# Depthwise convolution taps on rows that are not yet normalized, the wrapping strip first, and the last image's end in quarter blocks

## The chip, the cores and the metric

The kernel runs on one core of a Trainium2 chip. The metric is the device time of one execution in microseconds; the time before is the median of three runs, 4038.18 us (4037.26 to 4040.14). Everything is float32.

The engines are named as in the profile: PE (matrix products), PEld (its weight loads), DVE (vector), ACT (scalar, activation functions), POOL (GpSimd), SP (the queue that issues most DMAs). Each takes its instructions in the order in which the program emitted them, and stands still when the next one has to wait.

## The reference

The input `x` has 16 images of 56 x 56 pixels and 384 channels. Two residual layers follow each other:

```
x = x + window_attention(group_norm(x))       # 7x7 windows, shifted by 3, 12 heads of 32
x = x + depthwise_conv3x3(group_norm(x))      # per channel, zero padding, weights clipped to +-1, then their sign
```

The group norm takes mean and variance over the whole image for each of 32 groups of 12 channels, and has neither scale nor shift of its own. So the second layer of an image needs the attention output of all its rows before its norm is known. The attention rolls the image by 3 rows and columns, so that one strip of 7 rows wraps from the bottom of the image to its top, and masks the window pairs that the roll brought together.

## The kernel before

**Tiling.** Channels lie on the 128 partitions, three blocks of them (`NC = 3`). An image is 8 strips of 7 rows, 392 tokens each. A strip is two units of four windows, so there are 256 units `u`, 16 for an image; the loop is in `all_units` (L1013). Strip `r` of an image begins at row `7r + 3`; so the wrapping one (rows 52 to 55 and 0 to 2) is the last of its image.

**Attention of a unit.** Its heavy pieces are the list of `heavy` (L980): six pieces in each unit, three PE products each. Even units make the values of the next strip (`value`, L513, turned by DVE, L526) and half of its queries and keys (`query_key`, L499); odd ones make the other half, then the output projection of their strip (`project`, L690). Around these pieces lie, in this order of the unit: the sums of exponents (`add_up`, L639), logarithm and inverse on ACT (L678, L679), the product with the values (`attend`, L660), and DVE's divide group (L680, L681, L688). In the middle of the unit the scores of the next unit (L569), DVE's exponent input (`softmax`, L586) and ACT's exponential (L604) follow. The projection's result is added to `x` by DVE (L707), and its statistics for the second norm are taken (L713). PSUM has four banks of tag `mm` for all products and outputs and four for the scores.

**Order of the light work.** Loads, norms and convolution are not in that loop. A planner puts each of their pieces at a time counted in units, a fraction included: `at(when, f, ...)` (L942). The loop emits the pieces due, in order of time, behind the heavy piece whose sixth of the unit they fall into:

```
while light and light[0][0] - u <= (i + 1) / len(todo):
    _, g, a = light.pop(0)
    g(*a)
```

`plan_load` (L963) loads the next image: POOL issues its DMAs (`fetch_halves`, L449; a strip takes 12, the wrapping one 48), DVE turns the strip (L466), ACT sorts it into windows (L478, L481), DVE takes statistics (L482). At the image's end POOL works out its first norm (`norm_gather`, `norm_scale`), which passes through DRAM twice.

**The convolution of an image** runs beside the attention of the next, in six bands of 28 rows by 128 channels (`plan_conv`, L945). The projected rows of a strip go to DRAM (`mid`, 59 wide, issued by POOL, L723, after a small copy that wraps the columns, L719). When the last strip is done, the second norm is worked out on POOL and `center` (L730) turns it into coefficients. From 3 units behind the image's end, a band is taken up every 2.6 units: SP loads it (`band`, L741), ACT writes its normalized rows into a zero-bordered buffer (`pad`, L791) and the centre tap with the residual into an accumulator (`middle`, L821), DVE adds eight taps (`tap`, L827) and turns the sum in blocks of 32 (`turn_sum`, L834), SP stores it (`store`, L841). For the convolution that runs beside the last image the step is 1.95.

**The end.** The last image's convolution has no attention beside it. `plan_last` (L907) waits for its norm, worked out by products on PE (`norm_products`), and then gives four bands of the channel blocks 0 and 1 to DVE as above, and the third block to PE, in four quarters of 14 rows: `convolve` (L848) multiplies the normalized rows with diagonal matrices of the taps, 114 columns at a time, which turns them by token as well. `turn_late` (L887) turns the later DVE bands on PE, and their outputs are issued by SP and ACT.

Of the kernel before, what the change touches and what calls it, by code (L numbers as in the profile page):

```python
# [34 lines left out]
def kernel(  # L35
# [30 lines left out]
    R = W + SHIFT  # L66
    LT = 2 * W
# [17 lines left out]
    bpool = ctx.enter_context(tc.tile_pool(name="xb", bufs=1))  # L85
# [23 lines left out]
    dw_t = const.tile([P, NC, 9], F32, tag="dw", name="dw_t")  # L109
    bias = const.tile([P, 2, NH, 2, T], F32, tag="bias", name="bias")  # L110
# [13 lines left out]
    hps = [const.tile([P, BR + 2, W + 2], F32, tag=f"hp{n}", name=f"hp{n}") for n in range(2)]  # L124

    accs = [const.tile([P, 2 * BR, D], F32, tag=f"o{n}", name=f"o{n}") for n in range(2)]
# [22 lines left out]
    def clear_conv():  # L149
        for t in (*xls, *hps, *accs):  # L150
            nc.gpsimd.memset(t, 0.0)
# [42 lines left out]
    def load_depthwise():  # L194
# [10 lines left out]
        nc.vector.tensor_copy(dw_t, pw[:, : NC * 9].rearrange("p (c t) -> p c t", c=NC))  # L205

    loaded_bias = []

    def load_bias(queue, first_q, last_q, fast):


        if not loaded_bias:
            rel = ypool.tile([P, NC, WIN, R], F32, tag="y", name="rel").rearrange("q c h w -> q (c h w)")[:, : T * NH]
            nc.gpsimd.memset(rel, 0.0)
            loaded_bias.append(rel)
# [15 lines left out]
        mask = ypool.tile([P, NC, WIN, R], F32, tag="y", name="mask").rearrange("q c h w -> q (c h w)")[:, : 2 * T]  # L231
# [80 lines left out]
    def fetch_late():  # L312
# [3 lines left out]
        def place(name, rows, width, at=None):  # L316
# [7 lines left out]
        hp = [  # L324
            place("hp_late", LR + 2, W + 2, xls[1].rearrange("p t c -> p (t c)")),
            place("hp_late2", LR + 2, W + 2),
        ]
        acc = [
            place("acc_late", LR, W + 2, xt.rearrange("p c k d -> p (c k d)")),
            place("acc_late2", LR, W + 2),  # L330
        ]
        for t in (*hp, *acc):
            nc.gpsimd.memset(t, 0.0)
        late_tiles.update(gm=gm, dg=dg, hp=hp, acc=acc)
# [5 lines left out]
    def norm_products(key, gm, meanwhile=()):  # L340
        st = stats.pop(key)
# [24 lines left out]
        for f, n in meanwhile[:1]:  # L366
            f(n)
# [7 lines left out]
        for f, n in meanwhile[1:]:  # L375
            f(n)
# [10 lines left out]
    def late_norm(b):  # L387
        norm_products((1, b), late_tiles["gm"])

    xs = {}  # L390
# [5 lines left out]
    def fetch(s):  # L396
        b, r = divmod(s, NS)
        xl = staging(s)
        first = r * WIN + SHIFT
# [37 lines left out]
    def fetch_halves(s, c):  # L437
# [6 lines left out]
        first = r * WIN + SHIFT  # L444
# [133 lines left out]
    def softmax(u, fast):  # L578
# [4 lines left out]
        if fast:  # L583
# [6 lines left out]
            bias[:, int(s % NS == NS - 1)].rearrange("q (i j) w k -> q i (j w) k", i=HPC),  # L590
# [99 lines left out]
    def project(s, m):  # L690
# [4 lines left out]
        if m == 0:  # L695
            ys[s] = ypool.tile([P, NC, WIN, R], F32, tag="y", name=f"y_{s}")
# [9 lines left out]
        view = ys[s][:, m, :, SHIFT:R]  # L706
# [7 lines left out]
        if m == NC - 1:  # L714
            if b not in mids:
                mids[b] = dram.tile([P, NC, H, R], F32, tag="mid", name=f"mid_{b}")
            del xs[s]
            yt = ys.pop(s)
            nc.gpsimd.tensor_copy(yt[:, :, :, 0:SHIFT], yt[:, :, :, W:R])  # L719
            r0 = r * WIN + SHIFT  # L720
            n = min(WIN, H - r0)
            queue = nc.sync if s == B * NS - 1 else nc.gpsimd
            queue.dma_start(mids[b][:, :, r0 : r0 + n, :], yt[:, :, 0:n, :])  # L723
            if n < WIN:
                queue.dma_start(mids[b][:, :, 0 : WIN - n, :], yt[:, :, n:WIN, :])
# [4 lines left out]
    def center(b, pool=nc.gpsimd):  # L730

        coef = coefs[1, b]
        cen = small.tile([P, NC, 2], F32, tag="cen", name=f"cen_{b}")
        pool.tensor_tensor(cen[:, :, 0], coef[:, :, 0], bo_sb, ALU.mult)
        pool.tensor_tensor(coef[:, :, 1], coef[:, :, 1], cen[:, :, 0], ALU.add)
        pool.tensor_tensor(cen, coef, dw_t[:, :, 4].unsqueeze(2).to_broadcast([P, NC, 2]), ALU.mult)
        pool.tensor_scalar(cen[:, :, 0], cen[:, :, 0], 1.0, None, ALU.add)
        pool.tensor_tensor(cen[:, :, 1], cen[:, :, 1], bo_sb, ALU.add)
        centers[b] = cen

    def band(b, k, c):  # L741
# [3 lines left out]
        xb = bpool.tile([P, BR + 2, R], F32, tag="xb", name=f"xb_{b}_{k}_{c}")  # L745
        nc.sync.dma_start(xb[:, at : at + hi - lo, :], mids[b][:, c, lo:hi, :])
        bands[b, k, c] = (xb, at, hi - lo)

    last_strip = ((0, (NS * WIN + SHIFT) % H), ((NS - 1) * WIN + SHIFT, H))

    def band_late(b, k, c, part):

        rows = LR if c == NC - 1 else BR
        lo, hi = max(k * rows - 1, 0), min((k + 1) * rows + 1, H)
        first = k * rows - 1
        if part == 0:
            size = (rows + 2) * R
            if c == NC - 1:
                xb = xpool.tile([P, NC, ST], F32, tag="x", name=f"xb_late_{k}").rearrange("p c n -> p (c n)")
            elif (k, c) == (0, 1):  # L760
                xb = qk.rearrange("p m n -> p (m n)")
            elif (k, c) == (1, 0):
                xb = bias.rearrange("p v h w n -> p (v h w n)")
            else:
                xb = bpool.tile([P, BR + 2, R], F32, tag="xb", name=f"xb_{b}_{k}_{c}").rearrange("p h w -> p (h w)")
# [10 lines left out]
    def pad(b, k, c, late=False):  # L776
# [10 lines left out]
        if k == 0:  # L787
            nc.gpsimd.memset(hp[:, 0, :], 0.0)
# [385 lines left out]
```

## Time and profile before

| what | us |
|---|---|
| median of the runs shown | 4038.18 |
| the profiled execution's own time | 4038.97 |
| its span, first to last instruction | 4037.2 |
| PE busy | 3956.5 |
| DVE busy | 3494.4 |
| ACT busy | 2228.2 |
| POOL busy | 1863.1 |
| last mean of the second norm begins (L345) | at 3945.45 |

Busy time is the union of an engine's instructions. In a row of a timeline the first number is the start in us from the span's start, the second the time from the first to the last of the instructions merged in it; in brackets stand the idle time ahead of it and what ended it. In a row by stretches the engines' busy times stand in the order PE, PEld, DVE, ACT, POOL, then the granted clock of PE, the share of the DMA engines and GB/s.

### The profile page before, as it was taken

Reading aid. Unit: us, or ns where it says so; the run is one execution under the profiler, and the core shown is the slowest. Engines: PE = TensorE matmul, PEld = TensorE weight load, DVE = VectorE, ACT = ScalarE, POOL = GpSimd, SP = SyncE. Lnnn points to the kernel's source line nnn. Section 1 sums busy time; section 2 is a strip of 40 time slices with the busy share of each in tenths; the row PEclk is TensorE's granted clock in tenths of the full one; section 3 lists DMA queues with packets and bytes.
Section 4 is the critical chain, followed back from the end, with each engine's and each line's share of the span. In section 5 each row is a group of like instructions: output and inputs, shape, how many; then the busy total and the mean of one; then the engine's idle time right before and its main releaser. Section 6 shows DMA issues by size and latency. Waiting matters only on the chain.

```text
span 4037.2 us, 144682 instructions
## 1 busy us (share of the span) xinstructions
PE 3956.5 (98%) x63189; PEld 2416.3 (60%) x63189; DVE 3494.4 (87%) x3730; ACT 2228.2 (55%) x4678; POOL 1863.1 (46%) x3159
## 2 busy tenths in 40 slices
PE   7999999999999999999999999999999999999987
PEld 5665555555566565555655556565655655656657
DVE  4656989899898998989899898998989899898897
ACT  3545556556565655556556565655556556565542
POOL 5454545455453554545455453564545455452000
PEclk9999999999999999999999999999999999999998
DMA  4323545454554554545454554554545454553444
GB/s 106 79 70 87 116 104 120 105 126 103 113 120 101 124 113 103 116 104 122 105 126 104 114 119 100 125 112 103 115 109 118 106 124 107 111 119 81 114 104 104
DMA packets 802161, 439.35 MB, mean 109 GB/s; under 512 B 671478, under 2 KB 752023, under 8 KB 801518
## 3 DMA queue, kind: packets, MB, share of 16 engines
q1 hardware_dynamic: 712580, 270.46, 30.8%
q0 software_dynamic: 87648, 159.12, 16.6%
q8 instruction: 498, 8.16, 0.9%
q14 instruction: 145, 1.19, 0.1%
q10 hardware_dynamic: 1290, 0.42, 0.0%
HBM read 170.08 MB, written 158.45 MB: 81 GB/s over the span
## 4 chain that ended last, share of the span: by engine, by line
PE 38%; issue 19%; POOL 17%; DVE 14%; DMA 7%; ACT 2%; SPq 1%; DVEq 0%; POOLq 0%; ACTq 0%
PE pq L502 15%; POOL xl L449 12%; PE py L699 8%; PE pv L515 8%; DVE o L827 6%; PE score_banks L569 3%; PE po L660 2%; DMA mvd<-mv 2%; DMA xl<-in_x_dram 2%; PE score_banks L639 2%; DVE e L586 2%; DVE xt L466 1%; POOL dev L287 1%; DMA gt<-mvd 1%; DMA cod<-both 1%
## 5 line engine op out<-in xcount | busy, mean ns | idle before, releaser
L502 PE MATMUL pq<-xn,wq_t 128*128 128x392 f32 x4608 | 1584.9, 496 | 0.0
L449 POOL DMA_DIRECT2D xl<-in_x_dram x1980 | 1329.1, 726 | 148.0 <-DVE xt L466 96.2
L827 DVE SCALAR_TENSOR_TENSOR o<-hp,dw_t,o 128x1568 f32<-128x1568 f32 x752 | 1378.1, 1833 | 5.4
L502 PEld LDWEIGHTS pq<-xn,wq_t 128*128 128x128 f32 x4608 | 845.4, 188 | 595.9 <-ACT o L821 0.4
L515 PE MATMUL pv<-xn,wq_t 128*128 128x392 f32 x2304 | 815.0, 497 | 13.6 <-DVE y L707 13.6
L699 PE MATMUL py<-ot,wo_t 128*128 128x392 f32 x2304 | 817.9, 500 | 8.2 <-DVE ot L688 7.5
L509 ACT COPY qk<-pq 128x392 f32<-128x392 f32 x768 | 367.4, 482 | 565.5 <-PE pq L502 565.3
L719 POOL COPY y<-y 128x63 f32<-128x63 f32 x128 | 57.1, 446 | 1236.7 <-DVE y L707 1236.7
L699 PEld LDWEIGHTS py<-ot,wo_t 128*128 128x128 f32 x2304 | 425.0, 190 | 311.5 <-DVE ot L688 26.2
L515 PEld LDWEIGHTS pv<-xn,wq_t 128*128 128x128 f32 x2304 | 423.9, 188 | 312.9 <-DVE y L707 15.7
L604 ACT ACTIVATE e<-e 128x1176 f32<-128x1176 f32 x256 | 303.2, 1184 | 499.7 <-DVE e L586 498.8
L680 DVE SCALAR_TENSOR_TENSOR ln<-score_banks,inv 128x588 f32<-128x588 f32 x256 | 195.8, 765 | 322.6 <-ACT inv L679 321.9
L522 ACT COPY vt<-pv 128x392 f32<-128x392 f32 x384 | 188.6, 491 | 366.6 <-PE pv L515 365.9
L569 PEld LDWEIGHTS score_banks<-qk 32*49 32x49 f32 x24576 | 265.8, 118 | 145.3 <-issue 113.5
L586 DVE SCALAR_TENSOR_TENSOR e<-score_banks,bias 128x1176 f32<-128x1176 f32 x256 | 347.0, 1355 | 5.9 <-PE score_banks L569 5.9
L660 PEld LDWEIGHTS po<-e,v 49*32 49x32 f32 x24576 | 311.2, 105 | 51.6 <-issue 2.0
L478 ACT COPY x<-xt 128x196 f32<-128x196 f32 x720 | 225.5, 368 | 176.6 <-DVE xt L466 176.5
L660 PE MATMUL po<-e,v 49*32 49x49 f32 x24576 | 309.9, 212 | 1.0 <-issue 1.0
L569 PE MATMUL score_banks<-qk 32*49 32x49 f32 x24576 | 298.0, 218 | 3.1 <-DVE ln L680 3.1
L526 DVE STREAM_TRANSPOSE vq<-vt 128x512 f32<-128x512 f32 x384 | 265.5, 693 | 8.1 <-ACT vt L522 4.9
L491 ACT ACTIVATE xn<-x,coef 128x392 f32<-128x392 f32 x384 | 247.0, 711 | 4.4 <-DVE coef L381 4.4
L707 DVE TENSOR_TENSOR y<-py,x 128x392 f32<-128x392 f32 x384 | 213.2, 555 | 41.3 <-PE py L699 37.8
(174 smaller groups left out, 3307.6 us busy)
## 6 DMA issues: line engine op xcount, KB each, us to landing
v<-vq SPq DMA_DIRECT2D x2048, 48.0 KB
xb<-mid SPq DMA_DIRECT2D x90, 855.5 KB
out_dram<-o SPq DMA_DIRECT2D x736, 98.0 KB
mid<-y POOLq DMA_DIRECT2D x112, 619.5 KB
xl<-in_x_dram POOLq DMA_DIRECT2D x1260, 52.5 KB
mid<-y POOLq DMA_DIRECT2D x15, 354.0 KB
xl<-in_x_dram POOLq DMA_DIRECT2D x180, 28.0 KB
mid<-y POOLq DMA_DIRECT2D x15, 265.5 KB
```

What stands on the lines that cost most here:

```text
L449: nc.gpsimd.dma_start(xz[i * D + lo : i * D + hi, c, k : k + n, :], flat[token : token + n * (hi - lo)].rearrange("(k t) c -> t k c", k=n) ...
L491: nc.scalar.activation(xn[:, c, :, :T], xs[s][:, c, :].rearrange("p (w t) -> p w t", t=T), AF.Identity, bias=coef[:, c, 1:2], scale=coef[: ...
L502: nc.tensor.matmul(pq[:, :ST].rearrange("p (w t) -> p w t", t=T), wq_t[:, c, m * P : (m + 1) * P], xn[:, c, :, :T], start=(c == 0), stop=( ...
L509: nc.scalar.copy(qk[:, m, :ST], pq[:, :ST])
L515: nc.tensor.matmul(pv[:, :ST].rearrange("p (w t) -> p w t", t=T), wq_t[:, c, 2 * C + m * P : 2 * C + (m + 1) * P], xn[:, c, :, :T], start= ...
L526: nc.vector.transpose(vq[:, :, :, m].rearrange("p h n d -> p n h d"), vt[:, m].rearrange("p (n w) (j b) -> p n (w j) b", w=2, b=D),)
L569: nc.tensor.matmul(pp[row * HT : row * HT + rows, i, k0 : k0 + T], qk[part, NC * fast + j, q0 : q0 + rows], qk[part, NC * (not fast) + j, ...
L586: nc.vector.scalar_tensor_tensor(e, pp[:, :, : NC * 2 * T].rearrange("q i (n k) -> q i n k", k=T), QSCALE, bias[:, int(s % NS == NS - 1)]. ...
L604: nc.scalar.activation(flat, flat, AF.Exp, accum_out=reach[:, 0, u : u + 1])
L660: nc.tensor.matmul(po[w][i * D : (i + 1) * D, (2 * j + r) * T : (2 * j + r + 1) * T], vs[s][keys, i, n * 2 + r, j], by_head(u)[keys, i * N ...
L699: nc.tensor.matmul(py[:, :ST], wo_t[:, c, m * P : (m + 1) * P], ots[s][:, c, :], start=(c == 0), stop=(c == NC - 1),)
L827: nc.vector.scalar_tensor_tensor(acc, by_half(hp[:, dy : dy + BR, dx : dx + W]), dw_t[:, c, t : t + 1], acc, ALU.mult, ALU.add)
```

## The change

Three things change together.

**Taps before the norm.** A convolution of normalized rows is the norm's scale times the convolution of the raw rows, plus the shift times the sum of the taps that fall inside the image. So DVE now adds taps on the raw band, while the norm isn't known yet. `begin` (ACT) writes tap 0 times the raw rows, seven `tap`s follow on DVE, `middle` (ACT, in place in the band) puts in centre tap, residual and the constant, and `edges` (POOL, three small additions for each band) takes off the constants of the taps that fall outside the image. `finish` (DVE) adds the scaled sum to this and turns it, in one call. The rows in `mid` are now 60 wide with zero columns at both sides, so that the padded copy isn't needed; the band pool has two buffers for one, and there are three accumulators for two.

The first band of an image is now planned 1.3 units before the image's end, not 3 after it; centre, edges and finish come where the norm is ready (1.9 units after the end, or behind the taps). The step is 2.6 units, and 1.85 for the later bands beside the last image.

**The wrapping strip first.** Strip `r` now begins at row `7(r-1) + 3`, so the wrapping strip is the first of its image, and the first bands are complete before the image is. The mask goes with it (`s % NS == 0`), and so do the 48 DMA issues of its load.

**The end.** The last image's convolution is in quarters of 14 rows for all channel blocks. The taps of the first three quarters run before the last attention unit is done: blocks 0 and 1 on DVE, block 2 on PE, in 48 steps of 392 columns that are spread over gaps (17 of them planned in the last two units). The last strip isn't written to DRAM, but copied into the last quarter by ACT. What remains after the norm is centre, edges, finish or join, and the output of twelve pieces, each turned on PE and copied out by ACT, with the last quarter's taps in between.

At the start the tap sums for the edges are worked out by DVE (eight small instructions), and the weights are staged in other buffers.

```diff
     def norm_products(key, gm, meanwhile=()):
...
-        for f, n in meanwhile[1:]:
-            f(n)
+        for f, *args in meanwhile[1:]:
+            f(*args)
...
+    def first_row(s):
+        return (s % NS - 1) % NS * WIN + SHIFT
...
-            nc.gpsimd.tensor_copy(yt[:, :, :, 0:SHIFT], yt[:, :, :, W:R])
-            r0 = r * WIN + SHIFT
+            nc.gpsimd.tensor_copy(yt[:, :, :, 1 : 1 + SHIFT], yt[:, :, :, W + 1 :])
+            nc.gpsimd.memset(yt[:, :, :, 0 : W + 2 : W + 1], 0.0)
+            if s == B * NS - 1:
+                late_tiles["rows"] = yt
+                return
+            r0 = first_row(s)
...
+    def begin(b, k, c):
+
+        outs[b, k, c] = accs[count[0] % len(accs)]
+        count[0] += 1
+        xb = bands[b, k, c]
+        nc.scalar.activation(sum_of(b, k, c), by_half(xb[:, 0:BR, 0:W]), AF.Identity, scale=dw_t[:, c, 0:1])
...
+    def centered(b, c, xb, rows):
+
+        cen = centers[b][:, c]
+        here = xb[:, 1 : 1 + rows, 1 : 1 + W]
+        nc.scalar.activation(here, here, AF.Identity, bias=cen[:, 0:1], scale=cen[:, 9:10])
+
+    def edged(b, c, xb, rows, top, bottom):
...
+            nc.gpsimd.tensor_tensor(here, here, by.to_broadcast(shape), ALU.add)
+
+        put(xb[:, 1 : 1 + rows, 1 : 1 + W : W - 1], 3, [P, rows, 2])
+        for side, row, n in ((top, 1, 0), (bottom, rows, 1)):
+            if side:
+                put(xb[:, row, 1 : 1 + W], 1 + n, [P, W])
+                put(xb[:, row, 1 : 1 + W : W - 1], 5 + 2 * n, [P, 2])
...
+    def finish(b, k, c):
+
+        acc, xb = sum_of(b, k, c), bands.pop((b, k, c))
+        nc.vector.scalar_tensor_tensor(
+            acc, acc, coefs[1, b][:, c, 0:1], by_half(xb[:, 1 : 1 + BR, 1 : 1 + W]), ALU.mult, ALU.add
+        )
         flat = outs[b, k, c].rearrange("p h w -> p (h w)")
         nc.vector.transpose(flat, flat)
...
+        at(first - 1.7, convolve, 4)
+        at(first - 1.3, convolve, 9)
+        at(first - 0.9, convolve, 4)
...
+        next_(convolve, 4)
+        next_(norm_products, (1, B - 1), late_tiles, ((convolve, 2), (taps, 0, (1, 2, 3))))
+        next_(center, B - 1, nc.vector)
+        next_(convolve, 9)
...
     def plan_conv(p, first, step, lead, late, queue):
...
-        first += lead
-        for n in range(NB * NC):
+        whens = [first + lead]
+        for n in range(1, NB * NC):
+            whens.append(whens[-1] + (2.6 if n < 3 else step))
+        ready = first + 1.9
+        for n, when in enumerate(whens):
             k, c = divmod(n, NC)
-            when = first + step * n
-            at(max(when - 1.22 * step, first - lead + 0.5), band, p, k, c)
-            at(when - 0.35 * step, pad, p, k, c)
-            at(when - 0.25 * step, middle, p, k, c)
-            for i, t in enumerate((0, 1, 2, 3, 5, 6, 7, 8)):
-                at(when + step * i / 9, tap, p, k, c, t)
-            at(when + step * 8 / 9, turn_sum, p, k, c)
+            end = when + step * 7 / 8
+            fin = max(end + 0.75, ready + 0.5)
+            at(max([when - 1.22 * step] + [f + 0.05 for f in freed[-2:-1]]), band, p, k, c)
+            freed.append(fin)
+            at(when - 0.3 * step, begin, p, k, c)
+            for i, t in enumerate((1, 2, 3, 5, 6, 7, 8)):
+                at(when + step * i / 8, tap, p, k, c, t)
+            at(max(end + 0.25, ready), middle, p, k, c)
+            at(max(end + 0.3, ready + 0.05), edges, p, k, c)
+            at(fin, finish, p, k, c)
...
-            plan_conv(b - 1, NU * b, 2.6 if b < B - 1 else 1.95, 3, 0.4, nc.gpsimd)
+            plan_conv(b - 1, NU * b, 2.6 if b < B - 1 else 1.85, -1.3, 0.4, nc.gpsimd)
```

## The prediction

> **What bounds the kernel now.** I read the busy time by stretches first: two steady images, the last image, and the end after the last attention unit.
>
> ```profile
> 1243.00:1486.00 243.00, 241.19 (x3908) 145.06 (x3907) 219.75 (x230) 139.27 (x293) 118.94 (x206) 1.00 0.50 112
> 3200.00:3443.00 243.00, 241.60 (x3910) 145.25 (x3909) 220.27 (x232) 138.96 (x293) 123.06 (x207) 1.00 0.51 113
> 3686.00:3929.00 243.00, 235.33 (x3983) 142.62 (x3982) 219.78 (x208) 124.86 (x226) 28.04 (x54) 0.99 0.42 97
> 3946.00:4037.20 91.20, 70.76 (x562) 69.96 (x562) 69.45 (x59) 25.34 (x28) 2.56 (x8) 0.82 0.37 81
> ```
>
> The columns after the length are PE, PEld, DVE, ACT and POOL. In a steady image PE is busy 241 of 243 us, so the 14 middle images have at most some 2 us each to give. DVE is busy 220 of 243 us: it is second, with little room, and what matters is when its work comes. At the end nobody is full; 91 us pass there, and this is where the change can gain.
>
> Next the timeline of PE and of DVE over one odd unit (it starts at 2273.90, where the sums of exponents begin) and the start of the even one behind it.
>
> ```profile
> 2273.90 0.72 PE L639 MATMUL score_banks<-e,ones 49*32 49x294 f32 x16
> 2279.66 2.14 PE L699 MATMUL py<-ot,wo_t 128*128 128x392 f32 x6
> 2289.02 0.72 PE L639 MATMUL score_banks<-e,ones 49*32 49x294 f32 x16
> 2291.65 4.22 PE L515 MATMUL pv<-xn,wq_t 128*128 128x392 f32 x12 [0.97 <-DVE y L707]
> ```
>
> ```profile
> 2276.33 0.77 DVE L680 SCALAR_TENSOR_TENSOR ln<-score_banks,inv 128x588 f32<-128x588 f32 x1 [0.98 <-ACT inv L679]
> 2278.01 0.77 DVE L688 TENSOR_TENSOR ot<-ot,ln 128x588 f32<-128x588 f32 x1
> 2278.70 1.84 DVE L827 SCALAR_TENSOR_TENSOR o<-hp,dw_t,o 128x1568 f32<-128x1568 f32 x1
> 2280.46 1.67 DVE L466 STREAM_TRANSPOSE xt<-xl 128x1440 f32<-128x1440 f32 x1
> 2285.33 1.36 DVE L586 SCALAR_TENSOR_TENSOR e<-score_banks,bias 128x1176 f32<-128x1176 f32 x1
> 2291.04 0.56 DVE L707 TENSOR_TENSOR y<-py,x 128x392 f32<-128x392 f32 x1
> ```
>
> They give three times by which DVE must have done something, or PE stands. In an odd unit the divided output (L688) is wanted at +5.8 us, when the projection starts (2279.66). In an even unit the third y must be written at +1.6 us, since the second value product takes its bank; here it came at 2291.60, +2.6, and PE stood 0.97. In every unit the exponent input (L586) must start by about +12.4: it started at 2285.33, its exponential ended at 2288.0, and the next unit began at 2289.0 with 1.0 to spare. Over this image the unit lengths are 14.9 to 15.1 us, save 15.9, 15.7 and 16.1 in the units 2, 5 and 8: 2.7 us of such standing.
>
> **The change, steady state.** Per band the work stays: before, 8 taps, a transpose and two ACT passes; after, 7 taps, a scaling of the same shape in the finish, the transpose, and two ACT passes. DVE's total is unchanged: 0. What changes is **when**: the transpose (2.0) and the finish (1.8) come as one block of 3.8 us, 0.75 units behind the taps, and the taps lie 0.325 units apart, not 0.289. I set out DVE's queue with starts from the rows above: tap 1.8 (2278.70 to 2280.46; eight of one kind took 15.06, so up to 1.89), turn of a loaded strip 1.6, exponent input 1.3, divide group 2.4, v turn 0.65, y 0.57, statistics 0.5.
>
> Unit 3: the exponent input of unit 2 starts at +8; behind it finish 3.8, strip turn, v turn, two taps, two statistics make 12.0 with itself, so the divide starts at +4.9 and ends at +7.3: PE waits 1.5. Unit 4: +2.4, divide, two statistics, two v turns, a tap and a finish put the exponent input at 12.7: 0.3. Unit 5: two taps, v turn and strip turn behind a late exponent input end the divide at +6.95: 1.15. Unit 7: a finish ahead of it, 5.95 and then 12.7: 0.3. Unit 8: third y at +2.6: 1.0. Unit 10: finish, y, tap, y behind the input of unit 9 put the third y at +4.0: 2.4. Sum 6.65.
>
> Two waits come on top. ACT's centre pass of the first band is queued at +1.9 units, right behind the input copies that end at 2289.5, and needs all of the centre coefficients; these were ready only at 2292.2:
>
> ```profile
> 2290.28 0.89 POOL L734 TENSOR_TENSOR cen<-coef,bo_sb 128x3 f32<-128x3 f32 x1 [1.74 <-DMA coef<-cod]
> 2291.91 1.76 ACT L791 ACTIVATE hp<-xb,coef 128x1624 f32<-128x1624 f32 x1
> ```
>
> One tap fewer stands ahead of the mean on DVE, so I expect 2290.7; behind ACT wait the v copy and the logarithm, for which DVE's divide waits. The divide of unit 2 then starts 3.3 us late, and unit 3 pays between 0 and 3.3: I take 1.0. The edge additions of the fifth band are queued on POOL behind the next image's norm chain, and DVE's finish waits for them: 0 to 1.2 in unit 12, I take 0.5. So 8.15, less the 2.7 there now: **5.5 us per image**, bounds 4.0 and 8.5. Loads and a convolution meet in 14 images: **+77** (56 to 119).
>
> At nothing: the band loads (they land 4 to 6 us after their issue in the trace, and the tightest has 8 before ACT's first tap), the wider rows (60 for 59), and the wrapping strip's 48 POOL issues, which move to the image boundary, where POOL is idle (28 us, 0.59 each); were this cover gone, the y copies and edges behind them would be up to 28 us late. One rule speaks against the edges. Each band has three POOL additions. The nearest row is POOL's copy at the same place:
>
> ```profile
> L719 POOL COPY y<-y x128: 235/247/1881, 111.9 to 3945.0; 128x63 f32<-128x63 f32 x128
> ```
>
> Its mean is 446 ns, so three are 1.3 us, inside the 0.45 units (6.8 us) between edges and finish, with 1.7 of ACT's pass. The Trainium skill (SBUF — State Buffer, Who interferes with whom) says that a DVE instruction with two SBUF inputs and a GpSimd instruction that reads SBUF exclude each other for the whole instruction; the 1881 is about a tap's length, so the trace agrees. Were each edge to wait for a whole tap, three would take 6.2, the finish would be 1.1 late, and 84 finishes cost 92. By the row 0; I take the row.
>
> **The change, last image.** Units 240 to 256 now hold some 56 taps and 7.5 transposes. After: 38 taps, 6 finishes and 42 half-size taps. Half of 1833 is 0.92; from the 588-element row (765) 0.97: 0.97 taken. That is 133 for 117, so DVE is at 236 of 243. After the last divide 11 half taps (11 us) lie between and ahead of the last three y, where DVE stood idle: the mean of the last norm, now at 3945.45, comes 7 us later, and the bursts add 5. **+12** (3 to 20). The 17 early convolution steps (0.69 each, two records of 0.344) fill PE's standing time of units 254 and 255 (3.2, 6.4 and 3.0 us).
>
> **The change, end.** From mean to end it takes 91.7 us now:
>
> ```profile
> 3945.45 0.81 DVE L345 BATCH_NORM_AGGREGATE mv<-st 128x2 f32<-128x48 f32 x3
> 3955.20 0.16 DVE L735 TENSOR_TENSOR coef<-coef,cen 128x3 f32<-128x3 f32 x1
> 3958.02 15.06 DVE L827 SCALAR_TENSOR_TENSOR o<-hp,dw_t,o 128x1568 f32<-128x1568 f32 x8
> 4027.48 0.94 ACTq L905 DMA_DIRECT2D out_dram<-xo  x2
> ```
>
> 10 us of norm, four DVE bands of 17, outputs, 10 to the end. After, counted from the mean: coefficients at 10.1, centre at 11.3. PE does nine steps to 14.8, two outputs (1.75 each) to 18.4, eight steps to 23.9, four outputs to 31, the last eight steps to 36.5. Only then may ACT centre the third quarter's last channels in place; with the next pass and its edges the fourth quarter's first finish is at 40.8. Four taps and a join to 46.1, output 48.4, centre and edges 50.4, finish 51.5, five taps 56.7, centre, edges, finish 59.9, output 62.1, DMA and end 7; 2 more for edges that meet taps: 71. **-21** (-12 to -31). DVE alone would need 33, so the order across engines sets it.
>
> **Sum.** 4037.2 (span) + 77 + 12 - 21 = 4105; the start's eight small DVE instructions add at most 1.5 beside loads, taken as 0.5; the median is 1.0 above the span: **4107**.
>
> **Rivals.** (1) The bursts are absorbed, so it is **faster**: DVE waits for ACT's inverse 322 us in all, and any such wait that shortens soaks up a burst. Then 0 + 7 - 23 (edges short): 4022. It turns at 1.1 us per image, 16 over 14. (2) Edges and ACT's hold cost in full, 8.5 per image or more: 4037 + 119 - 9 + 1 = 4148. (3) The end does not shorten, since two banks are held by partial sums until the first join: 4037 + 77 + 12 + 1 = 4127. Against it: most outputs come after that join.
>
> **How the numbers follow.** Likeliest 0.62 (its own range 4065 to 4135), rival 1 0.22, (2) 0.07, (3) 0.04, and 0.05 for small costs that cancel the end's gain. A measurement can tell about 0.2%, 8 us. Faster 0.22, same 0.05, slower 0.73. Leaving out the tails beyond 4148 and some of rival 1: 4020 to 4148.
>
> **What would show it.** Units 3, 5 and 10 of each image longer than 15.1, with waits of the projection for L688's successor and of values for y; ACT waiting for POOL's centre once an image; an image of about 247 us; mean to end near 71. An image of 242 would show the likeliest wrong.

## The result

| what | before | after |
|---|---|---|
| median, us | 4037.72 (4036.82 to 4040.14, 4 runs) | 4140.64 (4138.24 to 4144.1, 4 runs) |
| span of the profiled execution, us | 4037.2 | 4142.3 |
| an image, mean of images 2 to 14, us | 242.0 | 250.0 |
| start of unit 240 to the last mean, us | 235.1 | 250.2 |
| last mean to the end, us | 91.7 | 65.9 |

The changed kernel is slower: 1.0252 of the time before, 95% interval 1.0239 to 1.0265. An image is counted from the first sum of exponents (L637) of its first unit to that of the next image; images and units of an image are counted from 0. The difference of the two spans, 105.1 us, divides into 1.3 at the start, 114.6 in the images 0 to 14 (2.3 of it in image 0), 15.1 up to the last mean, and -25.9 from there to the end.

The busy time by stretches, for one steady image (5), for the last image up to its mean, and for the end; columns as in the prediction.

```profile
1352.00:1602.00 250.00, 241.44 (x3904) 144.32 (x3903) 220.73 (x230) 137.40 (x292) 132.00 (x233) 1.00 0.48 110
3826.20:4076.40 250.20, 238.55 (x3791) 142.28 (x3790) 224.62 (x227) 118.61 (x219) 26.28 (x82) 0.98 0.40 101
4076.40:4142.30 65.90, 36.04 (x168) 25.36 (x168) 38.10 (x61) 26.41 (x42) 9.04 (x25) 0.75 0.28 75
```

PE has as much to do in an image as before (241 us), and DVE too (221 us for 220). The eight microseconds are PE standing still. What PE and its helpers wait for, in the view of waits (total, number, longest, in us), the changed kernel:

```profile
ACT x L476 <- DVE xt L464: 284.2, 114, 5.3
...
PE py L697 <- DVE ot L686: 74.7, 69, 1.9
...
ACT xb L783 <- DVE o L775: 35.5, 15, 2.9
...
DVE o L809 <- POOL xb L792: 28.6, 26, 2.8
...
PE pq L500 <- ACT qk L507: 18.2, 14, 1.8
...
PE score_banks L637 <- ACT e L602: 16.1, 28, 6.0
```

The first of PE's lines, the projection waiting for the divided output, was 7.5 us in all before. A wait of the query product for ACT's copy (L507) was not on the list before. Two lines are of a kind that the kernel before did not have: ACT's centre pass in place (L783) waits for the band's last tap, and DVE's finish (L809) waits for POOL's edges. The first of these two is in unit 11 of every image. In image 9 it looks like this (the unit starts at 2497.06 and the next one, without a wait of PE, at 2513.28):

```profile
2503.09 0.77 DVE L686 TENSOR_TENSOR ot<-ot,ln 128x588 f32<-128x588 f32 x1
2503.91 2.24 PE L697 MATMUL py<-ot,wo_t 128*128 128x392 f32 x6 [1.05 <-DVE ot L686]
2505.72 1.73 ACT L783 ACTIVATE xb<-xb,cen 128x1568 f32<-128x1568 f32 x1 [2.33 <-DVE o L775]
```

ACT begins to wait 6.3 us into the unit. The divide for which PE stands got its inverse from ACT before that, and PE waits for nothing more in this unit, so this wait of ACT costs PE nothing. The waits for edges lie in the units 12 and 14, 0.7 and 1.2 us per image.

By unit, mean of images 2 to 14, in us:

| unit | 2 | 3 | 5 | 7 | 8 | 9 | 10 | 11 | 13 | others |
|---|---|---|---|---|---|---|---|---|---|---|
| before | 16.0 | 15.1 | 15.6 | 15.1 | 15.1 | 15.5 | 14.9 | 15.1 | 15.0 | 14.9 to 15.1 |
| after | 14.9 | 18.8 | 16.3 | 16.0 | 15.0 | 15.2 | 15.7 | 16.4 | 16.2 | 14.9 to 15.3 |

Nearly half of the loss is unit 3. Here it is in image 9, from 2369.92 on, first PE:

```profile
2369.92 0.73 PE L637 MATMUL score_banks<-e,ones 49*32 49x294 f32 x16
...
2371.99 4.22 PE L500 MATMUL pq<-xn,wq_t 128*128 128x392 f32 x12 [0.40 <-ACT qk L507]
2378.08 3.28 PE L697 MATMUL py<-ot,wo_t 128*128 128x392 f32 x6 [1.88 <-DVE ot L686]
2381.29 1.47 PE L567 MATMUL score_banks<-qk 32*49 32x49 f32 x96
```

and DVE and ACT of the same unit, DVE from a little before its start:

```profile
2365.17 1.83 DVE L809 SCALAR_TENSOR_TENSOR o<-o,coef,xb 128x1568 f32<-128x1568 f32 x1
2367.04 2.05 DVE L813 STREAM_TRANSPOSE o<-o 128x1792 f32<-128x1792 f32 x1
2369.01 1.64 DVE L464 STREAM_TRANSPOSE xt<-xl 128x1440 f32<-128x1440 f32 x1
2370.57 0.67 DVE L524 STREAM_TRANSPOSE vq<-vt 128x512 f32<-128x512 f32 x1
2371.16 1.81 DVE L775 SCALAR_TENSOR_TENSOR o<-xb,dw_t,o 128x1568 f32<-128x1568 f32 x1
2372.88 1.03 DVE L480 BATCH_NORM_STATS2 st<-x 128x6 f32<-128x392 f32 x2
2373.83 1.83 DVE L775 SCALAR_TENSOR_TENSOR o<-xb,dw_t,o 128x1568 f32<-128x1568 f32 x1
2375.58 0.76 DVE L678 SCALAR_TENSOR_TENSOR ln<-score_banks,inv 128x588 f32<-128x588 f32 x1
...
2377.26 0.77 DVE L686 TENSOR_TENSOR ot<-ot,ln 128x588 f32<-128x588 f32 x1
```

```profile
2370.68 0.63 ACT L476 COPY x<-xt 128x196 f32<-128x196 f32 x2 [3.75 <-DVE xt L464]
2371.34 0.21 ACT L479 COPY x<-xt 128x21 f32<-128x21 f32 x1
2371.45 0.48 ACT L507 COPY qk<-pq 128x392 f32<-128x392 f32 x1
```

DVE is behind: a band's finish and transpose, 3.9 us, stand ahead of the strip turn that ACT wants, which is done only at 2370.6, and two taps and two statistics stand ahead of the divide, which ends 8.1 us after the unit's start, where 5.8 was the time by which PE wants it. ACT passes the lateness on by another way: its strip copies stand at the head of its queue for 3.75 us, and the query copy behind them, which frees a bank for PE, comes late too (PE's waits in unit 3 are 1.75 us for the divide and 1.26 for that copy, mean of images 2 to 14).

### The profile page after: what moved, and what is told of

Read it like the earlier page. It is cut to its first block, busy times and chain, and to the rows that moved or that the text cites. A ratio compares the mean times of both kernels' runs of the same rounds, so it can differ in the third digit from the quotient of the medians.

```text
span 4142.3 us, 144415 instructions
## 1 busy us (share of the span) xinstructions
PE 3963.5 (96%) x62837; PEld 2380.3 (57%) x62837; DVE 3526.0 (85%) x3780; ACT 2217.3 (54%) x4698; POOL 2008.5 (48%) x3591
## 3 DMA queue, kind: packets, MB, share of 16 engines
q0 software_dynamic: 87680, 160.49, 16.2%
## 4 chain that ended last, share of the span: by engine, by line
DVE 32%; PE 31%; issue 11%; DMA 8%; POOL 7%; ACT 7%; SPq 2%; DVEq 0%; POOLq 0%; ACTq 0%
DVE o L775 10%; PE pq L500 9%; PE py L697 9%; PE pv L513 6%; DMA xl<-in_x_dram 3%; DVE xt L464 3%; DVE e L584 3%; DVE o L809 3%; PE score_banks L567 2%; POOL xl L447 2%; DVE vq L524 2%; DVE st L480 2%; DVE ln L679 2%; DVE st L711 2%; PE po L658 2%
## 5 line engine op out<-in xcount | busy, mean ns | idle before, releaser
L500 PE MATMUL pq<-xn,wq_t 128*128 128x392 f32 x4608 | 1588.3, 497 | 18.4 <-ACT qk L507 18.2
L500 PEld LDWEIGHTS pq<-xn,wq_t 128*128 128x128 f32 x4608 | 847.0, 188 | 617.0 <-ACT qk L507 20.6
L775 DVE SCALAR_TENSOR_TENSOR o<-xb,dw_t,o 128x1568 f32<-128x1568 f32 x630 | 1157.1, 1837 | 1.8
L697 PE MATMUL py<-ot,wo_t 128*128 128x392 f32 x2304 | 827.4, 504 | 77.1 <-DVE ot L686 74.7
L507 ACT COPY qk<-pq 128x392 f32<-128x392 f32 x768 | 359.3, 483 | 546.1 <-PE pq L500 545.9
L717 POOL COPY y<-y 128x63 f32<-128x63 f32 x128 | 33.5, 262 | 796.0 <-DVE y L705 796.0
L480 DVE BATCH_NORM_STATS2 st<-x 128x6 f32<-128x392 f32 x360 | 199.7, 560 | 81.9 <-ACT x L479 81.5
L792 POOL TENSOR_TENSOR xb<-xb,cen 128x56 f32<-128x56 f32 (+1 forms) x270 | 156.8, 581 | 226.9 <-ACT xb L783 212.4
```

The lines of the kernel that those rows point to most:

```text
L480: nc.vector.bn_stats(stats[0, b][:, c, r, :], xs[s][:, c, :])
L500: nc.tensor.matmul(pq[:, :ST].rearrange("p (w t) -> p w t", t=T), wq_t[:, c, m * P : (m + 1) * P], xn[:, c, :, :T], start=(c == 0), stop=( ...
L507: nc.scalar.copy(qk[:, m, :ST], pq[:, :ST])
L697: nc.tensor.matmul(py[:, :ST], wo_t[:, c, m * P : (m + 1) * P], ots[s][:, c, :], start=(c == 0), stop=(c == NC - 1),)
L775: nc.vector.scalar_tensor_tensor(acc, by_half(xb[:, dy : dy + BR, dx : dx + W]), dw_t[:, c, t : t + 1], acc, ALU.mult, ALU.add)
```

## Experiments: which part of the change costs

All times are medians; ratios are to the kernel before, run on the same chip beside each group of experiments (4038.6 to 4039.0). The first four undo or isolate one part each.

**The wrapping strip first, alone, in the kernel before.**

```diff
+    def first_row(s):
+        return (s % NS - 1) % NS * WIN + SHIFT
...
-        first = r * WIN + SHIFT
+        first = first_row(s)
...
-            bias[:, int(s % NS == NS - 1)]
+            bias[:, int(s % NS == 0)]
```

> The kernel before, with the wrapping strip first and nothing else changed: its load with 48 issues moves on POOL's queue from the middle of the image to its end, and the mask with it. Queue theory: DVE's order does not change, so 4034 to 4042. Theory of the wrapping strip (the load stands in the way of what POOL and ACT do at the image's end): a good part of the 8 us per image, 4070 to 4140.

Measured: 4039.2, ratio 1.0001 (0.9992 to 1.0010); an image takes 242.1 us. Moving the strip, its mask and its 48 POOL issues costs nothing that can be measured.

**The edges left out.**

```diff
-            at(max(end + 0.3, ready + 0.05), edges, p, k, c)
```

> The changed kernel, with the three edge additions on POOL left out for all bands that run beside attention (those of the end stay), so the output is wrong at the image borders. POOL theory (edges and DVE shut each other out, and the finish waits for them): most of the 8 us per image goes, 4030 to 4070. Queue theory: only the fifth band's wait behind the norm chain goes, some 1 us in units 12 and 13 of 14 images, so 4115 to 4135, and unit 3 stays near 18.8 us.

Measured: 4130.02, ratio 1.0224 (1.0207 to 1.0241); an image 249.2 us. The edges are worth some 10 of the 103 us (0.8 us per image; the intervals of the two ratios just overlap, so the size is rough). In this trace no finish of the bands beside attention waits for POOL or for ACT, and yet unit 3 takes 18.9 us, and PE's wait for the divide is what it was:

```profile
PE py L697 <- DVE ot L686: 72.2, 70, 1.9
```

So at least 7.2 of the 8.0 us per image are not a wait of DVE for the edges or the centre pass.

**Finish and transpose apart.**

```diff
             at(fin, finish, p, k, c)
+            at(fin + 0.3, turn_sum, p, k, c)
```

> The changed kernel, with the block transpose taken out of the finish and planned 0.3 units behind it, so that other DVE work can come between the two. Queue theory (what counts is how much DVE work stands between two deadlines of PE, not whether it is in one piece): most of the sum stays on the same side of the same deadlines, so 249 to 251 us per image and 4125 to 4155 in all. Block theory (the 3.8 us in one piece is what holds the divide and the exponent input): 243 to 245 per image, 4050 to 4075. POOL theory (the edge additions hold DVE): no change, 4141.

Measured: 4148.0, ratio 1.0267 (1.0250 to 1.0285); an image 250.6, unit 3 even 19.7. The block of 3.8 us as such isn't it.

**DVE's work spread evenly.** Taps 0.289 units apart as before the change, the finish 0.52 units behind the last tap (1.08 in the change), the transpose 0.26 units behind it, and all bands at equal distances. The run also moves the first band, from 1.3 units ahead of the image's end to 0.7 behind it, and the centre pass, from 0.5 to 0.3 units ahead of the finish.

```diff
-        whens = [first + lead]
-        for n in range(1, NB * NC):
-            whens.append(whens[-1] + (2.6 if n < 3 else step))
+        whens = [first + lead + step * n for n in range(NB * NC)]
...
-            fin = max(end + 0.75, ready + 0.5)
+            fin = max(when + 2.25 * step / 2.6, first + 2.4)
...
+            at(fin + step / 10, turn_sum, p, k, c)
```

> The changed kernel, with the steady bands planned at nine even places as before the change: seven taps 0.289 units apart, the finish at the eighth place, the transpose alone at the ninth, the first band 0.7 units after the image's end (0.1 beside the last image, step 1.9). Queue theory: unit lengths as before the change, 241 to 244 us per image; beside the last image DVE has more to do, so the end gains little: 4025 to 4050. POOL theory and theory of the wrapping strip: edges and order of strips are as in the changed kernel, so still 248 to 251 per image and 4125 to 4150.

Measured: 4108.23, ratio 1.0173 (1.0156 to 1.0190); an image 247.0. A third of the loss goes, two thirds stay. So the order of DVE's work matters, but a queue that is only badly ordered would have given much more. One thing got worse here: ACT waits 56.0 us for last taps at the centre pass, for 35.5 in the changed kernel. In this run unit 9 is the longest (17.9 us), with waits of PE for ACT's query copy; that pointed at ACT.

## Experiments: is it ACT that passes the loss on?

**ACT's strip copies later,** in the changed kernel and in the spread one. The first norm's exchange on POOL had to move with them, since it needs their statistics.

```diff
-                at(when + 0.2 + 0.2 * c, arrange, s, c)
+                at(when + 0.6 + 0.2 * c, arrange, s, c)
...
-        at(when + 0.8, norm_gather, (0, b), nc.gpsimd)
-        at(when + 0.9, norm_scale, (0, b), nc.gpsimd)
+        at(when + 1.05, norm_gather, (0, b), nc.gpsimd)
+        at(when + 1.15, norm_scale, (0, b), nc.gpsimd)
```

> The changed kernel with one edit: ACT's copies of a turned input strip are issued 0.4 units (6 us) later, so that they no longer stand at the head of ACT's queue while DVE's strip turn is late; DVE's order is not touched. If a good part of the loss reaches PE through ACT (the copies wait for the strip turn, the query and key copies and the logarithm wait behind them), the waits of the projection products for ACT's query copy go, unit 3 shrinks from 18.8 us to 17.0 to 17.5 and the time is 4100 to 4128. If DVE's queue alone sets the loss, the divide comes no earlier and the time stays within 8 us of the changed kernel: 4133 to 4149.

> The spread order of the experiment before (taps, finish and transpose at even distances, 4108) with ACT's copies of a strip 0.4 units later as well. If what was left there is the relay through ACT (unit 9 mainly: 2.9 us per image), the time is 4060 to 4085 and unit 9 falls from 17.9 us to below 16. If DVE's queue alone sets it, 4100 to 4116.

Measured: 4237.59 (1.0491, 1.0473 to 1.0508) and 4221.55 (1.0452, 1.0431 to 1.0472). Neither theory had that. In the first of the two, PE's waits for the query copy are gone, as meant, but the projection's wait for the divide grew (78.0 us in all for 74.7, the longest 2.8 for 1.9) and unit 3 stays at 18.6: there the relay through ACT took nothing that DVE's lateness would not have taken. Most of the hundred microseconds on top are another matter: unit 12 takes 20.6 us, for 15.2 before the edit, 5.4 in each image. The timeline of image 9, unit 12 of this run, POOL and DVE:

```profile
2575.76 0.79 POOL L313 DMA_DIRECT2D coef<-cod  x1 [1.37 <-DMA cod<-both]
2576.58 0.95 POOL L792 TENSOR_TENSOR xb<-xb,cen 128x56 f32<-128x56 f32 x3
```

```profile
2577.56 1.85 DVE L809 SCALAR_TENSOR_TENSOR o<-o,coef,xb 128x1568 f32<-128x1568 f32 x1 [6.72 <-POOL xb L792]
2579.44 2.04 DVE L813 STREAM_TRANSPOSE o<-o 128x1792 f32<-128x1792 f32 x1
2581.41 1.26 DVE L524 STREAM_TRANSPOSE vq<-vt 128x512 f32<-128x512 f32 x2
2582.60 1.34 DVE L584 SCALAR_TENSOR_TENSOR e<-score_banks,bias 128x1176 f32<-128x1176 f32 x1
```

The fifth band's edges stand on POOL behind the norm exchange of the next image. Moved back by a quarter of a unit and with later statistics, that exchange ends so late that DVE's finish stands 6.72 us for the edges; the exponent input behind it starts at 2582.60, 18.4 us into the unit, and PE stands 6.13. In the changed kernel the same wait is 0.82 us long. In the spread order with late copies DVE waits for edges 188.9 us in all.

## Experiments: the centre pass in place

**DVE in the order of the kernel before.** Bands at the former phase, the finish where the eighth tap was, the transpose where it was; everything else as in the changed kernel. A second run had ACT's copies late as well.

```diff
-            fin = max(when + 2.25 * step / 2.6, first + 2.4)
+            fin = max(when + step * 7 / 9, first + 2.4)
...
-            at(max(fin - 0.3, first + 1.9), middle, p, k, c)
+            at(max(fin - 0.2, first + 1.9), middle, p, k, c)
...
-            at(fin + step / 10, turn_sum, p, k, c)
+            at(fin + step / 9, turn_sum, p, k, c)
...
-            plan_conv(b - 1, NU * b, 2.6 if b < B - 1 else 1.9, 0.7 if b < B - 1 else 0.1, ...)
+            plan_conv(b - 1, NU * b, 2.6 if b < B - 1 else 1.9, 0.4 if b < B - 1 else 0.1, ...)
```

(The lines with a minus are those of the spread run.)

> DVE gets the order of the kernel before: bands at the same phase, seven taps 0.289 units apart, the finish where the eighth tap was, the transpose behind it. ACT's centre pass stays in place, 0.2 units ahead of the finish. If the order of DVE's work is the whole loss of the steady state, an image takes 242 to 243.5 us again and the time is 4025 to 4050, below the kernel before by the gain at the end. If the centre pass in place costs by itself (ACT waits for the last tap of the band, and what is queued on ACT behind it waits too), an image takes 245 to 247 us and the time is 4065 to 4095, with PE waits for ACT's copies in the units of a last tap.

> The run with DVE's former order, and ACT's copies of a strip 0.4 units later. With that order the strip turn comes when it came before the change, so the queue theory expects no difference to that run beyond 8 us. The theory that ACT relays the loss expects a gain of 10 to 30 us, if that run still shows PE waits for ACT's query and key copies behind the strip copies.

Measured: 4145.93 (1.0265, 1.0248 to 1.0282) and 4154.12 (1.0284, 1.0267 to 1.0301). An image takes 248.9 us with the very order that gave 242.0 before. So the former order does not give the former time as long as the centre pass is in place; the second theory was right in kind, and too small in size. But the loss is no longer the changed kernel's: it has moved to the units 0, 5, 7, 8 and 15, and unit 3 is at 15.3. Image 9, unit 15 of the first of the two, from 2549.19 on; ACT, POOL, DVE and PE:

```profile
2555.93 1.72 ACT L783 ACTIVATE xb<-xb,cen 128x1568 f32<-128x1568 f32 x1 [2.23 <-DVE o L775]
```

```profile
2555.89 3.55 POOL L447 DMA_DIRECT2D xl<-in_x_dram  x5 [0.39 <-DMA mid<-y]
2559.46 1.02 POOL L792 TENSOR_TENSOR xb<-xb,cen 128x56 f32<-128x56 f32 x3
```

```profile
2553.99 1.85 DVE L775 SCALAR_TENSOR_TENSOR o<-xb,dw_t,o 128x1568 f32<-128x1568 f32 x1
2560.52 1.85 DVE L809 SCALAR_TENSOR_TENSOR o<-o,coef,xb 128x1568 f32<-128x1568 f32 x1 [4.68 <-POOL xb L792]
...
2563.37 1.36 DVE L584 SCALAR_TENSOR_TENSOR e<-score_banks,bias 128x1176 f32<-128x1176 f32 x1
```

```profile
2566.10 0.73 PE L637 MATMUL score_banks<-e,ones 49*32 49x294 f32 x16 [1.47 <-ACT e L602]
```

This is the chain that the change made: the last tap ends on DVE, only then may ACT centre the rows in the buffer that the tap has read, only then may POOL put in the edges (and here it is in the middle of issuing loads), only then may DVE finish. From the tap's end at 2555.8 to the finish DVE stands 4.68 us, and everything behind the finish with it: the exponent input starts 14.2 us into the unit. In all, ACT waits 121.3 us for last taps in this run and DVE 125.5 us for edges (35.5 and 28.6 in the changed kernel). So this run shows what the chain costs when the finish stands close behind the taps; it does not show that the changed kernel pays for it.

The second run, with ACT's copies late, is 8.2 us slower than the first, at the edge of the 8 us that the queue theory allowed. The gain of 10 to 30 us that the relay through ACT would have given did not come.

**The centre pass into a tile of its own.** To take away what makes it wait, ACT writes the centred rows into the third sum tile; the edges go there, and the finish reads it. Two sum tiles are left. The pass is issued 0.6 units ahead of the finish, beside the taps, rather than 0.2 to 0.3; the tile and the earlier issue, which needs it, were not run apart. First with DVE's former order:

```diff
-        outs[b, k, c] = accs[count[0] % len(accs)]
+        outs[b, k, c] = accs[count[0] % 2]
...
-        centered(b, c, bands[b, k, c], BR)
+        nc.scalar.activation(aside, here, AF.Identity, bias=cen[:, 0:1], scale=cen[:, 9:10])
...
-            acc, acc, coefs[1, b][:, c, 0:1], by_half(xb[:, 1 : 1 + BR, 1 : 1 + W]), ALU.mult, ALU.add
+            acc, acc, coefs[1, b][:, c, 0:1], by_half(aside), ALU.mult, ALU.add
...
-            at(max(fin - 0.2, first + 1.9), middle, p, k, c)
-            at(max(fin - 0.15, first + 1.95), edges, p, k, c)
+            at(max(fin - 0.6, first + 1.9), middle, p, k, c)
+            at(max(fin - 0.55, first + 1.95), edges, p, k, c)
```

> DVE's order of the kernel before, as in the run with that order, but ACT's centre pass writes a tile of its own (the third sum tile, so two sums are left, as before the change), and pass and edges are issued 0.6 units ahead of the finish, without waiting for the band's last tap. If the loss that the former order left (248.9 us per image) is the chain last tap, centre pass in place on ACT, edges on POOL, finish on DVE, with each engine's queue standing behind it, an image takes 242 to 244 us, ACT no longer waits for a tap at the centre pass, and the time is 4025 to 4055. If the loss is something else (the extra POOL work, the rows not normalized, the transfers), the image stays at 247 to 250 us and the time at 4120 to 4155.

Measured: 4041.45, ratio 1.0006 (0.9996 to 1.0015). An image takes 241.6 us, for 248.9 with the pass in place; ACT waits for no tap at the centre pass. (In this run the third band of image 14's convolution takes over its sum tile before the last two stores of the first band, so a part of that one image's output is lost; the instructions are the same.) What kept it from being faster than before is the last image, where it takes 250.2 us from the start of unit 240 to that of unit 255 (220.5 before the change): ACT's first term of a sum waited up to 15.4 us until the store of an earlier sum from that tile was done.

**The same in the changed kernel's own order.** The edit is the same, without the two planned times.

> The changed kernel, its own order kept, with the centre pass written to a tile of its own in the same way: pass and edges no longer need the last tap, but they keep their place in the queues. The late finish with the transpose in one block stays. If the order of DVE's work is what costs in the changed kernel, and the wait of ACT's centre pass there (35.5 us in all, unit 11) only a small part, the image falls from 250.0 to 247 to 249.5 us and the time is 4105 to 4138. If the chain through ACT and POOL is the larger part in that order too, the time is 4040 to 4095.

Measured: 4715.74, ratio 1.1679 (1.1659 to 1.1698). This run doesn't decide what it was made for: with the late finish two sum tiles are too few, and ACT stood behind the stores for most of the difference.

```profile
ACT o L769 <- DMA out_dram<-o: 627.8, 63, 15.4
```

(Here the third sum of each image starts before the first one is wholly stored, so a part of the output is lost in every image.) ACT's stops are in the units 3, 6, 11 and 14 of an image. Where there are none, the trace tells something all the same: unit 5 takes 16.3 us and PE waits 0.89 us there for the divide, both as in the changed kernel, though the centre pass waits for no tap. The run also shows why the change needs a third sum tile: with the finish 0.75 units behind the taps, sum, finish, transpose and store together can outlast two bands.

**Own tile in the steady images, in place beside the last image,** with three sums there; with DVE's former order, and with the spread order.

```diff
+            if late_form:
+                gap, end = step / 8, when + step * 7 / 8
+                fin, put = max(end + 0.75, first + 2.4), max(end + 0.25, first + 1.9)
+            else:
+                gap, fin = step / 9, max(when + step * 7 / 9, first + 2.4)
+                put = max(fin - 0.6, first + 1.9)
```

(The second run has `when + 2.25 * step / 2.6` in place of `when + step * 7 / 9`.)

> Images 0 to 13: DVE's order of the kernel before, centre pass into the third sum tile, as in the run before. Image 14, whose convolution runs in the last image beside the early pieces of the last one: the changed kernel's form, centre in place and three sum tiles in rotation, since with two tiles the first term of a sum stood up to 15 us behind the store of the sum before it. With 241.6 us per image, 231 to 238 for units 240 to 255 and 84.7 behind unit 255: 82 + 3625 + 235 + 85 = 4027 and 1 for the median, 4018 to 4040, so faster than the kernel before by some 0.3%. If the steady images owed their 241.6 us to what they got wrong in no part, but the sums of the pieces don't hold (the last image keeps 250), 4040 to 4048.

> As the run above, but with the spread order on DVE (247.0 us per image with the centre in place) instead of the order of the kernel before. If what that order still lost came from the chain through ACT and POOL (centre waits for the last tap, finish for the edges), an image takes 241.5 to 243.5 us and the time is 4022 to 4055. If it came from where DVE's work lies, the image stays at 245.5 to 247.5 and the time is 4085 to 4115.

Measured: 4047.41 (1.0022, 1.0013 to 1.0032) and 4051.72 (1.0034, 1.0022 to 1.0046). The steady images hold in both orders: 241.6 and 242.3 us. Unit 15 of image 9 again, now from 2482.41 on, in the first of the two, POOL and DVE:

```profile
2486.09 3.05 POOL L794 TENSOR_TENSOR o<-o,cen 128x56 f32<-128x56 f32 x3
```

```profile
2487.22 1.87 DVE L775 SCALAR_TENSOR_TENSOR o<-xb,dw_t,o 128x1568 f32<-128x1568 f32 x1
2489.20 1.85 DVE L815 SCALAR_TENSOR_TENSOR o<-o,coef,o 128x1568 f32<-128x1568 f32 x1
...
2492.05 1.37 DVE L584 SCALAR_TENSOR_TENSOR e<-score_banks,bias 128x1176 f32<-128x1176 f32 x1
```

DVE's order is that of the run before with the pass in place, but the edges run beside the last tap and end with it (at 2489.14 and 2489.09), and the finish follows without a gap worth naming. The exponent input starts 9.6 us into the unit rather than 14.2.

The whole is no gain all the same: from the start of unit 240 to that of unit 255 it takes 254.1 and 248.7 us (231.1 in the changed kernel, 220.5 before it). In unit 241 ACT's first term of a band's sum stands 14.2 and 15.8 us, in the second run by the profile behind the store of an earlier sum: the last image's bands now follow closer on the bands before them. The sum of the parts, before's steady images with after's end, was expected at 4027 and has not been reached; whether another plan for the last image reaches it was not tried.

The steady state in one table, us per image (242.0 before the change):

| DVE's order | centre in place | centre in its own tile |
|---|---|---|
| of the change (finish 0.75 units late, in a block) | 250.0 | not measured free of the sum tiles |
| spread | 247.0 | 242.3 |
| of the kernel before | 248.9 | 241.6 |

## Why the prediction was right, and where it was not

The time lies in the range, and the sign and the shape (steady state loses, the end gains) are as forecast. The sum was 33.6 us short, nearly all in one term.

- **Steady state, 77.** Measured 112 in the images 1 to 14, 8.0 each and not 5.5; inside the bounds (56 to 119), near their upper end. The deadlines of DVE to PE that the prediction named are those at which PE stands. But its list of units is half right: unit 3 loses 3.7 us (2.5 with ACT's hold in it were charged), unit 4 0.4 (0.3), unit 5 is 1.3 over an undisturbed 15.0 (1.15), units 7 and 10 lose about 0.9 and 0.8 (0.3 and 2.4), unit 8 nothing (1.0); units 11 and 13, with 1.3 and 1.1, were not on it. The 16.1 us of unit 8 before the change were an exception of the image that the prediction read (image 9); in the images beside it that unit takes 14.9.
- **The cause under it** is the one named, DVE's work coming in bursts, and it was charged too low. Without the edges no finish waits in the steady state and an image still takes 249.2 us; ACT's wait for the last tap, in unit 11, lies behind the divide that PE wants. So about 7.2 of the 8.0 are bursts, for which the sum had 4.0 (6.65 less 2.7) and 1.0 for ACT's hold. In unit 3 the waits also came by a way that the sum did not have, ACT's strip copies with the query copy behind them. What exactly makes the bursts is open: the 3.8 us block alone does not (split, an image takes 250.6), and in the spread order, which gives back 3.0 with the pass in place and 7.7 with a tile of its own, the tap distances, the later finish and the place of the bands change together.
- **Two ACT passes for two, at nothing.** For the changed kernel this came out nearly right, but it was luck: the prediction had seen the pass in place as a serial step at the end, and did not ask for it in the steady state. There it is a chain over three queues between two of DVE's instructions. The finish planned 0.75 units late keeps that chain from standing and pays with bursts; closer, the bursts go and the chain stands, 4.7 us per image in the spread order (247.0 to 242.3) and 7.3 in the former one (248.9 to 241.6).
- **ACT's hold for the coefficients**, 1.0 of unit 3, bounds 0 to 3.3: ACT waits for them in 12 images, 0.9 us each and 1.1 at most, and nothing shows that PE pays: unit 2 takes 14.9 us, and in image 9, where ACT does not wait for them, unit 3 is as long as elsewhere. ACT held PE in another way, its strip copies behind a late strip turn; the run with late copies in the changed order, where unit 3 keeps its length, says that there this only passed on what DVE owed.
- **The edges, at nothing:** some 10 us. The row gave 0; an estimate from the rule of the Trainium skill (SBUF — State Buffer, Who interferes with whom), with a whole tap of waiting for each edge, gave 92; the row was the nearer. One edge takes 581 ns in the mean, for 446 of the row taken. The trace agrees with the rule for a part of them: 64 of the 270 edges take over 0.7 us, all of these beside a tap, and the others take 0.30 in the mean. In the run with the own tile, three edges beside a divide step and a tap took 3.05 us, 1.63 of it the third one, which ends with the tap; the same three took 1.02 in the run where no tap ran beside them, the third 0.20.
- **The edges behind the norm exchange, 0.5 in unit 12:** there, 0.82 us in image 9, and unit 12 is 0.3 us longer than before. The runs with late copies show the same place at 6.72: the cover that the prediction asked for is a quarter of a unit wide.
- **The wrapping strip, at nothing:** right, 4039.2 for 4038.7.
- **The last image, 12:** 15.1. Half a tap takes 1.03 us, not 0.97; over 42 of them that would be 2.5 of the 3.1.
- **The end, -21:** -25.9. The coefficients came 9.2 us after the mean (10.1 charged), PE's last steps ended at 31.1 (36.5), since four outputs ahead of them took PE 3.2 us and not 7.1, so the third quarter's last centre pass began at 31.2, and the last finish ended at 53.7 (59.9). The mean, a coefficient, and the last piece's chain:

```profile
4076.43 0.83 DVE L343 BATCH_NORM_AGGREGATE mv<-st 128x2 f32<-128x48 f32 x3
...
4085.47 0.17 DVE L736 TENSOR_TENSOR coef<-coef,cen 128x3 f32<-128x3 f32 x1
...
4121.64 5.31 DVE L869 SCALAR_TENSOR_TENSOR o<-wq_t,dw_t,o 128x784 f32<-128x784 f32 x5
4127.04 1.05 ACT L783 ACTIVATE wq_t<-wq_t,cen 128x784 f32<-128x784 f32 x1 [3.01 <-DVE o L869]
...
4129.13 1.04 DVE L882 SCALAR_TENSOR_TENSOR wq_t<-o,coef,wq_t 128x784 f32<-128x784 f32 x1 [2.18 <-POOL wq_t L792]
```

- **The rivals.** The first (bursts absorbed, 4022) is refuted: an image is 250 us. The second (4148) is the nearest in time, by other means: its hold is small and free for PE, and its edges cost a tenth of what it took. The third (the end does not shorten) is refuted by 65.9 us for 91.7.

## What to carry to other kernels

A pass in place looks free when instructions and busy times are counted, but it binds its start to the last reader of the buffer; where reader, pass, correction and user sit on three in-order queues, the price is the time in which the first engine stands with everything queued behind it. Here moving the user later hid the chain, in an order that made bursts; so first take away the need to wait (another buffer), then choose the order. And a wait that is new in the profile is not yet the cause: leave out what it waits for, and see whether the time follows (here 10 of 103 us). And ask of each moved instruction what stands ahead of it on its new queue: a norm exchange a quarter of a unit later on POOL, with later statistics, was worth 5.4 us per image here.

## What the hardware showed beyond this

After some of PE's waits of 1.7 to 1.9 us the granted clock falls to half for 3.4 us, in the middle of the steady state: five times in the changed kernel (at 375.5, 1123.0, 2130.0, 2379.1 and 3379.2 us), and never between 86 and 3922 us in the kernel before. The wait of 1.88 us in image 9 was followed by such a stretch, the equal wait in image 5 was not:

```profile
1379.42 2.24 PE L697 MATMUL py<-ot,wo_t 128*128 128x392 f32 x6 [1.88 <-DVE ot L686]
1381.59 1.20 PE L567 MATMUL score_banks<-qk 32*49 32x49 f32 x96
```

There the six projection products took 2.24 us and the scores 1.20; in image 9, shown above, 3.28 and 1.47, so the second price of such a wait is about 1.3 us. The Trainium skill (TensorE: Matmul & The Clock Gate, Part 1) states the fall after an idle window of some 3.4 us; here waits of about half that were enough at times.
